# A two-layer graph kernel on one core: stores moved to the load queue, sums of B kept in memory, a third scale spread by TensorE

## The chip, the core and the metric

The kernel runs on one core of a Trainium2 chip. The metric is the device time of one execution in microseconds; the time given is the median of several runs. One execution was also taken by the hardware profiler, and the views below come from it. Engines are named as in the profile: PE is TensorE's matmul, PEld its weight load, DVE is VectorE, ACT ScalarE, POOL GpSimd and SP SyncE. The last three and the DMA engines matter here mostly through their queues[...].

## The reference, cut to what matters

```python
def _L0_gnn_ref(cur, incidence_m):
    head = (incidence_m > 0).astype(incidence_m.dtype)
    head = head / jnp.maximum(jnp.sqrt(jnp.sum(head * head, axis=-1, keepdims=True)), 1e-12)
    inc = incidence_m + head
    return (inc @ cur) / jnp.sum(inc, axis=-1, keepdims=True)

def _L1_gnn_ref(X, A, W):
    A2 = A + jnp.eye(A.shape[0], dtype=A.dtype)
    dscale = jnp.diagonal(A2) ** (-0.5)
    temp = A2 @ X @ W.T
    A_norm = dscale[:, None] * A2 * dscale[None, :]
    return jax.nn.relu(A_norm @ temp)

x = _layernorm(x + _L0_gnn_ref(x, adj))          # x: 4096 x 512, adj: 4096 x 4096, float32
x = _layernorm(x + _L1_gnn_ref(x, adj, L1_gnn_W))
```

Three large products have adj as one factor: inc @ x in layer 0, then A2 @ X and A_norm @ temp in layer 1. For layer 0 every row of adj needs the number of its positive elements before it can be used: its square root scales the 0/1 mask that is added.

## The kernel before, in words

**Stage 1, layer 0** (lines 602 to 689). The rows of adj are taken in pairs of row blocks, j and j + 16, of 128 rows each. A pair runs through four chunks (c = 0 to 3) of the other dimension. Each 2x2 arrangement of blocks is multiplied by Strassen's scheme in Winograd's form: seven products instead of eight, from sums of the four quarters. `prepare1` makes a chunk ready on VectorE one chunk ahead: raw sums for the later layers (`raw_sums`), the mask times its scale (`masks`, L449, and L456), the sums (`add_up`, L168 to L171). `multiply1` (L487) issues the 28 products of the chunk. At the end of a pair `combine` takes the seven results out of their banks, the first copies of it by ScalarE (L518, L524).

The counts are ScalarE's. `count(times)` takes that many tiles (128 x 512 elements of adj in natural order), lets `signs` (L337) add up the signs of each, for pairs from 4 on also a plain sum (L385), and asks for a further tile on SP's queue (`load_natural`, L372; five buffers). One pair has 16 tiles. How many are counted behind which chunk is written out by hand, in the tuple that `count` is given in the loop over the chunks. When a pair's 16 counts are there, `spread` makes them into a scale that lies along the free dimension: part 0 adds up and takes the root; after it there are two ways. Parts 1 and 2 multiply the identity by it on VectorE (L407) and let TensorE spread it with a matrix of ones (L422), and ScalarE copies the result out (L424). Part 3 instead stores it in DRAM and loads it back to all partitions, both on POOL's queue (L415, L417). Before the change the scales of pairs 1 and 2 go TensorE's way, pair 1's in the opening and pair 2's while pair 1 is multiplied; all later ones go by DRAM.

**Stages 2 and 3, layer 1** (from L1041). Both products, k = 2 and k = 3, are cut by Strassen's scheme twice: an outer one with seven products p, and within each an inner one of seven matmuls. So `steps` runs over k, two strips s, the seven p in the order of ORDER, and eight kk: 224 steps, each of seven matmuls (`multiply2`, L283), each matmul two instructions in the trace. Eight steps with one p are called a phase here. For each step VectorE sums the adj side (`prepare`, L168 to L171, three buffers) two steps ahead, and for every two steps (a group) it makes the inner sums of the B side (`sum_b`):

```python
t = pools["tops"].tile([P, 2, 4, P], F32, name="ts", bufs=2)
nc.vector.tensor_sub(t[:, :, 0:2, :], ...)              # L262
nc.vector.scalar_tensor_tensor(t[:, :, 2, :], ...)      # L263
nc.vector.tensor_add(t[:, :, 3, :], ...)                # L264
```

The tile of adj sums, a, is loaded by SP (`load`, L214 to L218) LA + PF steps ahead (three in k = 2, five in k = 3) into a ring of four or six buffers; the raw B, tr, is loaded by SP too (`load_b`, L255, three buffers), after every second step.

Outer sums of adj that k = 2 makes and k = 3 needs again are stored in DRAM. S1 and S3 come from layer 0. S2 and S4 are made in `prepare` of k = 2, in phases p = 6 and p = 3, from a tile r that stays in memory for the strip: `tensor_add(r, r, a)` (L237) for the last four kk, at `raises` (L249) earlier for the first four. Each is then stored by POOL's queue (L238), 1 MB, 32 times.

At the end of a phase `outer` takes the seven results out (L702 to L710). While k = 2 still runs, `project` multiplies finished row pairs by W (L784), sums the parts into rows z (L813 to L822), and `leave_operands` scales them and stores them by POOL (L837, L843) as the B side of k = 3. In k = 3 `layer1` and `layer1_first` turn finished blocks back (L858), rectify them (L862, L906), add the residual and take statistics in `rest`, one step later. `finish` then works off the last four steps by product instead of by step (L936), so that each result can be taken out while the next is multiplied.

Of the kernel before, what the change touches and what calls it, by code (L numbers as in the profile page):

```python
# [13 lines left out]
P = 128  # L14
# [12 lines left out]
def tile_adj_resnorm_d2(  # L27
# [158 lines left out]
    RAISES = {1: A11, 2: A12, 6: A11, 3: A12}  # L186
    EARLY = NQ // 2

    DONE = {(2, 7): 1, (2, 3): 0, (3, 6): 0, (3, 4): 1}
    steps = [(k, s, p, kk) for k in (2, 3) for s in range(NS) for p in ORDER[k] for kk in range(NQ)]  # L190
    groups = [st[:3] + (st[3] // 2,) for st in steps[::2]]
# [2 lines left out]
    resident, loaded, ready, raw_b, sums_b = {}, {}, {}, {}, {}  # L194
    made = {"a": 0, "s": 0, "load": 0, "load_b": 0}
    going, leaving = [], []
    queue, pairs, later, deferred, raises = [], [], [], [], []

    def fresh():

# [28 lines left out]
    def prepare(n):  # L229
        k, s, p, kk = steps[n]  # L230
        for i in range(n, len(steps) if n == len(steps) - TAIL + 1 else n + 1):
            complete(i)
        a = loaded.pop(n, None)
        r = resident[kk] if k == 2 and p != 4 and p != 7 else None
        if k == 2 and p in (3, 6):
            if a is not None:
                nc.vector.tensor_add(r, r, a)  # L237
            nc.gpsimd.dma_start(out=outer_2[s, kk, S2 if p == 6 else S4], in_=r)  # L238
            a = r
        i = made["s"]  # L240
        made["s"] += 1
        if n < len(steps) - 2:
            sm = (work, pools["work"], work)[i % 3].tile([P, 4, SW], F32, tag="s", name="s")
        else:

            sm = C_of[3][0][n - len(steps) + 2]
        add_up(sm, a)
        if k == 2 and p in (1, 2) and kk < EARLY:
            raises.append(lambda: nc.vector.tensor_add(r, r, a))  # L249
        ready[n] = a, sm  # L250
# [7 lines left out]
    def sum_b(g):  # L258

        b = raw_b[g]  # L260
        t = pools["tops"].tile([P, 2, 4, P], F32, name="ts", bufs=2)
        nc.vector.tensor_sub(t[:, :, 0:2, :], b[:, :, 0:4:3, :], b[:, :, 1:2, :].to_broadcast([P, 2, 2, P]))  # L262
        nc.vector.scalar_tensor_tensor(t[:, :, 2, :], t[:, :, 0, :], -1.0, b[:, :, 3, :], op0=ALU.mult, op1=ALU.subtract)  # L263
        nc.vector.tensor_add(t[:, :, 3, :], b[:, :, 2, :], t[:, :, 2, :])  # L264
        sums_b[g] = t

    def factors(n):

# [16 lines left out]
    def load_up_to(n):  # L285
        while made["load"] <= min(n, len(steps) - 1):
            load(made["load"])
            made["load"] += 1
# [86 lines left out]
    def count(times):  # L375
        for _ in range(times):
            if not waiting:
                return
            (j, h, t), nat = waiting.pop(0)
            if j not in counts:  # L380
                counts[j] = w1_pool.tile([P, 2, NT], F32, name="cnt")
                if j >= SUMMED:
                    totals[j] = w1_pool.tile([P, 2, NT], F32, name="tot")
            if j >= SUMMED:
                nc.scalar.activation(nat, nat, AF.Copy, accum_out=totals[j][:, h, t:t + 1])  # L385
            signs(nat, nat, counts[j][:, h, t:t + 1])
            load_natural()
# [76 lines left out]
    def prepare1(n, between=None):  # L464
        if n not in early:
            raw_sums(n, between)
        sums[n] = work.tile([P, 4, CW], F32, tag="s", name="s")
        for h in range(2):
            to_inc(n, h)
        add_up(sums[n], chunks[n])  # L470
# [177 lines left out]
    for n in range(NC, NP * NC):  # L648
        j, c = divmod(n, NC)
        if c == 0:  # L650
            if j > 1:
                C = combine(j - 1, acc)
            acc = [bank(m) for m in range(7)]
        if n + 2 >= NP * NC:
            load_up_to(n + 2 - NP * NC)
        else:
            load_chunk(n + 2)
        scales = j < NP - 1 and c == (2 if j == 1 else 1)
        if scales:
            spread(j + 1, 0)  # L660
        if n + 1 < NP * NC:
            prepare1(n + 1, between=(lambda: spread(j + 1, 1 if j == 1 else 3)) if scales else None)
        else:
            prepare(0)
        if n == NC:
            for g in range(5, NP // 2):
                build_last(g)
        multiply1(n, acc, (lambda: spread(j + 1, 2)) if scales and j == 1 else None)
        count(((6, 6, 5, 6) if j == 1 else (5, 4, 5, 2))[c])
        if j == 1 and c == 1:  # L670
            nc.vector.tensor_scalar(dscale, dscale, 1.0, None, op0=ALU.add)
            nc.scalar.activation(dscale, dscale, AF.Sqrt)
            nc.vector.reciprocal(dscale, dscale)
            nc.gpsimd.tensor_scalar(nscale, dscale, -1.0, None, op0=ALU.mult)
        if c == 1:
            layer0(j - 1, C)
        elif c == 2:
            operands(j - 1, C)
        if c == 3:
            load_rows(j)  # L680
# [367 lines left out]
    for n, (k, s, p, kk) in enumerate(steps):  # L1048
        if kk == 0:
            acc = [bank(m) for m in range(7)]  # L1050
        load_up_to(n + LA + PF)
        if n + LA < len(steps):
            prepare(n + LA)
        if n % 2 == 0 and n // 2 + 1 < len(groups):
            sum_b(n // 2 + 1)
        end = n >= len(steps) - NQ
        items = [queue.pop(0) for _ in range(min(len(queue), 2 if end else 1))] if 1 <= kk <= (6 if end else 5) else []
        held = later[:]
        later.clear()
        while deferred:  # L1060
            deferred.pop(0)()
            if not pairs:
                break
        between = {3: lambda: take_up(items.pop(0))} if len(items) > 1 else {}
        if kk in (2, 4) and pairs:
            going.append(project(*pairs.pop(0), kk == 2))
        for pair in going:
            between.update(next(pair))
        if kk == 5 and leaving:

            between[2], between[4] = leaving
            leaving.clear()
        if n < len(steps) - TAIL:
            multiply2(n, acc, between)
        if n == 0:
            layer0(NP - 1, C)
        elif n == 1:
            operands(NP - 1, C)
            parts = w_t.rearrange("(f e p) (o d) -> f o p e d", e=2, p=P, o=2)
            for op, (f, o) in {B11: (0, 0), T4: (0, 1), B21: (1, 0), B22: (1, 1)}.items():  # L1080
                nc.gpsimd.dma_start(out=wt[:, op], in_=parts[f, o])
        elif n == 4:
            outer_sums(wt[:, T1:T4 + 1], wt[:, B11], wt[:, T4], wt[:, B21], wt[:, B22])
        if n % 2 == 1 and n > 1:
            load_b_up_to(n // 2 + 3)
        for item in items:
            take_up(item)
        for rest in held:
            rest()
        for pair in going[::-1]:  # L1090
            next(pair)
        if kk in (4, 6):
            del going[:1]
        if 1 <= kk <= (6 if end else 5):
            for kind, args in queue[:2]:
                fetch(kind, *args)
        if kk == NQ - 1 and n + 1 < len(steps):
            outer(k, p, acc)
            if (k, p) in DONE:
                h = DONE[k, p]  # L1100
                if k == 2:
                    pairs.extend((h, s, i) for i in range(SB))
                else:
                    queue.extend((layer1, (h, b)) for b in blocks(h, s))
            if n == len(steps) - 1 - NQ:
                last = sorted(blocks(1, s), key=lambda b: b[1])
                queue.extend((layer1_first, (1, *last[i:i + 2])) for i in range(0, len(last), 2))
            for kind, args in queue[:2]:
                fetch(kind, *args)
        while raises:  # L1110
            raises.pop(0)()
        while kk == NQ - 1 and leaving:
            leaving.pop(0)()
        if n + 1 == len(steps) // 2:

            scope.close()
            ring3 = ctx.enter_context(tc.tile_pool(name="ring3", bufs=2))
            late["pool"] = ctx.enter_context(tc.tile_pool(name="late", bufs=1))

            root, eps_by = (late["pool"].tile([P, NB], F32, name=t) for t in ("root", "eps_by"))  # L1120
            nc.vector.reciprocal(root, dscale)
            nc.vector.scalar_tensor_tensor(eps_by, root, LN_EPS, root, op0=ALU.mult, op1=ALU.mult)
            late["root"], late["eps"] = root, eps_by
            i = made["a"] % 4
            pools["turn"] = [ring3] * 2 + pools["turn"][i:] + pools["turn"][:i]
            made["a"] = 0
            PF = 3
# [36 lines left out]
```

## Time and profile before

| | |
|---|---|
| median of 3 runs | 2284.97 us (2283.08 to 2285.19) |
| profiled execution, its own time | 2280.52 us |
| its span | 2278.7 us |
| PE busy | 2253.0 us, 99% |
| DVE busy | 1858.3 us, 82% |
| ACT busy | 536.3 us, 24% |
| POOL busy | 354.3 us, 16% |
| SP's DMA queue | 417.38 MB |
| POOL's DMA queue | 137.03 MB |

The span runs from the first to the last instruction of the core; the execution's own time has a little around it. Busy times of engines overlap, so they don't add up to the span. In the lists of waits a line reads: the engine and the tile and line that waited, the engine and line that released it, the total in us, how often, and the longest. In timelines: start, duration, engine, line, operation, what is written from what, the shapes, the count, and in brackets the idle time ahead of it with its releaser. In the tables by window each engine has its busy time and, in brackets, its number of instructions; after them come the granted clock of TensorE, the busy share of the DMA engines and the GB/s that they moved.

### The profile page before, as it was taken

The page shows a single profiled execution, that of the slowest core. Times are in us where ns is not written, and L with a number is a line of the kernel's source. Part 1 is how long each engine was busy: PE and PEld are TensorE (multiplying, and loading weights), DVE is VectorE, ACT ScalarE, POOL GpSimd, SP SyncE. Part 2 cuts the span into 40 slices and gives each one's busy share as a digit, 9 for nine tenths or more (in the row PEclk, how much of TensorE's full clock was granted, in tenths as well). Part 3 has the DMA queues.
Part 4 walks back from the last instruction along what each step waited for, and adds up shares of the span by engine and source line. Part 5 has one row for each costly group of instructions (what it writes and reads, how often), then busy time and mean ns, then how long its engine had stood idle before and what let it go on. Part 6 is the DMA issues. An engine that isn't in the chain of part 4 may idle for free.

```text
span 2278.7 us, 22117 instructions
## 1 busy us (share of the span) xinstructions
PE 2253.0 (99%) x7358; PEld 1382.7 (61%) x7359; DVE 1858.3 (82%) x2635; ACT 536.3 (24%) x1335; POOL 354.3 (16%) x500
## 2 busy tenths in 40 slices
PE   8999999999999999999999999999999999999997
PEld 6888888888888844445555444555544444444443
DVE  6988998989899787789876778887767788767787
ACT  4345545545553000000111100111110011100013
POOL 0111112211121110001333300233320000000010
PEclk9999999999999999999999999999999999999999
DMA  9787778878776576574766856577785576766572
GB/s 329 274 298 249 254 258 265 271 257 271 249 250 219 192 284 241 210 268 183 289 240 212 285 202 257 193 288 258 224 254 218 217 259 243 261 231 225 215 259 105
DMA packets 155425, 555.80 MB, mean 244 GB/s; under 512 B 17408, under 2 KB 31760, under 8 KB 116912
## 3 DMA queue, kind: packets, MB, share of 16 engines
q1 hardware_dynamic: 114624, 417.38, 51.9%
q0 software_dynamic: 40688, 137.03, 17.7%
q8 instruction: 58, 0.95, 0.2%
q14 instruction: 55, 0.45, 0.1%
HBM read 434.78 MB, written 119.55 MB: 243 GB/s over the span
## 4 chain that ended last, share of the span: by engine, by line
PE 92%; DMA 3%; DVE 3%; ACT 1%; issue 0%; SPq 0%; POOL 0%; DVEq 0%; ACTq 0%
PE q L283 56%; PE q L487 31%; PE q L784 4%; DMA nat<-adj 1%; DMA b<-x 1%; PE q L936 1%; DMA a<-adj_q 1%; DMA ob<-z 1%; ACT nat L337 0%; DVE s L168 0%; PE q L858 0%; DVE s L170 0%; DVE o L713 0%; DVE st L150 0%; DVE c L713 0%
## 5 line engine op out<-in xcount | busy, mean ns | idle before, releaser
L283 PE MATMUL q<-s,ts 128*128 128x512 f32 x1320 | 609.4, 592 | 0.0
L487 PE MATMUL q<-b,s 128*128 128x256 f32 (+1 forms) x1920 | 453.7, 379 | 0.3 <-DVE s L170 0.3
L283 PEld LDWEIGHTS q<-s,ts 128*128 128x128 f32 x1320 | 250.9, 190 | 296.8 <-issue 270.0
L168 DVE TENSOR_TENSOR s<-a 128x1024 f32<-128x1024 f32 x234 | 288.1, 1231 | 148.9 <-PE q L283 122.1
L487 PEld LDWEIGHTS q<-b,s 128*128 128x128 f32 x1920 | 363.0, 189 | 52.4 <-DVE s L170 0.7
L487 PE MATMUL q<-b,a 128*128 128x256 f32 (+1 forms) x1440 | 350.8, 379 | 1.4 <-ACT p L518 1.4
L283 PE MATMUL q<-a,tr 128*128 128x512 f32 x688 | 327.7, 593 | 2.2 <-DVE c L703 2.2
L487 PEld LDWEIGHTS q<-b,a 128*128 128x128 f32 x1440 | 272.9, 190 | 40.0 <-ACT p L518 1.9
L283 PE MATMUL q<-s,tr 128*128 128x512 f32 x440 | 224.7, 592 | 0.0
L283 PEld LDWEIGHTS q<-a,tr 128*128 128x128 f32 x688 | 129.0, 190 | 144.8 <-issue 136.6
L337 ACT ACTIVATE nat<-nat,tiny 128x512 f32<-128x512 f32 x240 | 172.9, 721 | 33.7 <-DMA nat<-adj 27.3
L283 PE MATMUL q<-a,ts 128*128 128x512 f32 x344 | 175.8, 593 | 0.0
L170 DVE TENSOR_TENSOR s<-a,s 128x512 f32<-128x512 f32 x234 | 165.6, 708 | 8.0
L171 DVE TENSOR_TENSOR s<-a,s 128x512 f32<-128x512 f32 x234 | 165.3, 706 | 8.0
L702 ACT COPY p<-q 128x512 f32<-128x512 f32 x27 | 15.7, 583 | 652.6 <-PE q L283 642.5
L449 DVE SCALAR_TENSOR_TENSOR mask<-a,sc 128x1024 f32<-128x1024 f32 (+2 forms) x129 | 154.2, 1196 | 2.1
L456 DVE TENSOR_TENSOR a<-a,mask 128x1024 f32<-128x1024 f32 x123 | 150.7, 1225 | 6.2
L283 PEld LDWEIGHTS q<-s,tr 128*128 128x128 f32 x440 | 83.7, 190 | 91.5 <-issue 82.4
L385 ACT ACTIVATE nat<-nat 128x512 f32<-128x512 f32 x192 | 118.3, 616 | 21.3 <-DMA nat<-adj 21.2
L283 PEld LDWEIGHTS q<-a,ts 128*128 128x128 f32 x344 | 65.4, 190 | 82.4 <-issue 76.9
L439 POOL DMA_DIRECT2D oa<-sr x64 | 57.7, 902 | 276.3 <-DVE sr L430 176.4
L891 POOL DMA_DIRECT2D out<-o x24 | 13.1, 545 | 532.2 <-ACT o L163 532.2
(216 smaller groups left out, 2223.9 us busy)
## 6 DMA issues: line engine op xcount, KB each, us to landing
a<-adj_r SPq DMA_DIRECT2D x112, 1024.0 KB, 6.8
a<-oa SPq DMA_DIRECT2D x80, 1024.0 KB, 5.3
nat<-adj SPq DMA_DIRECT2D x240, 256.0 KB, 6.1
a<-adj_q SPq DMA_DIRECT2D x60, 1024.0 KB, 6.1
tr<-ob SPq DMA_DIRECT2D x112, 512.0 KB, 3.9
oa<-sr POOLq DMA_DIRECT2D x64, 512.0 KB, 7.1
oa<-r POOLq DMA_DIRECT2D x32, 1024.0 KB, 9.1
y<-x POOLq DMA_DIRECT2D x64, 256.0 KB, 7.7
```

Of the source, the lines that this page charges most:

```text
L168: nc.vector.tensor_add(s[:, S3:S1 + 1, :], a[:, A11:A22 + 1, :], a[:, A21, :].unsqueeze(1).to_broadcast([P, 2, w]))
L170: nc.vector.tensor_add(s[:, S2, :], a[:, A11, :], s[:, S1, :])
L171: nc.vector.tensor_add(s[:, S4, :], a[:, A12, :], s[:, S2, :])
L283: nc.tensor.matmul(acc[m], left, right, start=(kk == 0), stop=(kk == NQ - 1))
L337: nc.scalar.activation(y, a, AF.Sign, bias=tiny, scale=2.0 ** 64, accum_out=accum)
L385: nc.scalar.activation(nat, nat, AF.Copy, accum_out=totals[j][:, h, t:t + 1])
L439: nc.gpsimd.dma_start(out=dst, in_=sr.rearrange("p m (k i) -> p (m k) i", i=P))
L449: nc.vector.scalar_tensor_tensor(m, v, 0.0, s.unsqueeze(1).to_broadcast(list(v.shape)), op0=ALU.is_gt, op1=ALU.mult)
L456: nc.vector.tensor_add(z, z, y)
L487: nc.tensor.matmul(acc[m][:, 0:w], left, b[:, right, 0:w], start=(kk == 0), stop=(kk == NP - 1))
L784: nc.tensor.matmul(ps, left[:, e, :], wt[:, right, e, :], start=(e == 0), stop=(e == 1))
L936: nc.tensor.matmul(acc[m], left, right, start=False, stop=(kk == NQ - 1))
```

## The change

It has three parts.

1. In `prepare` of k = 2 the store of S2 or S4 is no longer issued on POOL's queue at once. It is put on a list, and the next step issues it on SP's queue, after that step's load of a.
2. In `sum_b`, for the phases p = 7 and p = 4 of k = 3 (the last two in the order), the first strip stores its inner sums of B in DRAM (on POOL's queue, eight tiles of 512 KB), and the second strip loads them (on SP's queue) instead of making them on VectorE.
3. The scale of pair 3, made while pair 2 is multiplied, goes TensorE's way as that of pair 2 does, one chunk later than before (c = 2). The counts are dealt out anew: 6, 6, 5, 2 in pair 1, 5, 4, 6, 3 in pair 2, 7, 4, 5, 2 in pair 3, and 5, 4, 5, 2 from then on; before they were 6, 6, 5, 6 in pair 1 and 5, 4, 5, 2 from then on.

```diff
+    KEPT = (7, 4)
+    kept_b = {}
...
-            nc.gpsimd.dma_start(out=outer_2[s, kk, S2 if p == 6 else S4], in_=r)
+            stores.append(lambda: nc.sync.dma_start(out=outer_2[s, kk, S2 if p == 6 else S4], in_=r))
             a = r
...
         t = pools["tops"].tile([P, 2, 4, P], F32, name="ts", bufs=2)
+        k, s, p, i = groups[g]
+        sums_b[g] = t
+        if (k, s) == (3, NS - 1) and p in KEPT:
+            nc.sync.dma_start(out=t, in_=kept_b[p, i])
+            return
         nc.vector.tensor_sub(t[:, :, 0:2, :], b[:, :, 0:4:3, :], b[:, :, 1:2, :].to_broadcast([P, 2, 2, P]))
         nc.vector.scalar_tensor_tensor(t[:, :, 2, :], t[:, :, 0, :], -1.0, b[:, :, 3, :], op0=ALU.mult, op1=ALU.subtract)
         nc.vector.tensor_add(t[:, :, 3, :], b[:, :, 2, :], t[:, :, 2, :])
-        sums_b[g] = t
+        if (k, s) == (3, 0) and p in KEPT:
+            kept_b[p, i] = dram.tile([P, 2, 4, P], F32, name=f"kb{p}_{i}")
+            nc.gpsimd.dma_start(out=kept_b[p, i], in_=t)
...
-        scales = j < NP - 1 and c == (2 if j == 1 else 1)
+        scales = j < NP - 1 and c == (2 if j <= 2 else 1)
         if scales:
             spread(j + 1, 0)
         if n + 1 < NP * NC:
-            prepare1(n + 1, between=(lambda: spread(j + 1, 1 if j == 1 else 3)) if scales else None)
+            prepare1(n + 1, between=(lambda: spread(j + 1, 1 if j <= 2 else 3)) if scales else None)
...
-        multiply1(n, acc, (lambda: spread(j + 1, 2)) if scales and j == 1 else None)
-        count(((6, 6, 5, 6) if j == 1 else (5, 4, 5, 2))[c])
+        multiply1(n, acc, (lambda: spread(j + 1, 2)) if scales and j <= 2 else None)
+        count({1: (6, 6, 5, 2), 2: (5, 4, 6, 3), 3: (7, 4, 5, 2)}.get(j, (5, 4, 5, 2))[c])
...
         load_up_to(n + LA + PF)
+        while stores:
+            stores.pop(0)()
         if n + LA < len(steps):
             prepare(n + LA)
```

More of the change, by code (lines that the diff above doesn't have):

```diff
@@ L196, in tile_adj_resnorm_d2 @@
     going, leaving = [], []
-    queue, pairs, later, deferred, raises = [], [], [], [], []
+    queue, pairs, later, deferred, raises, stores = [], [], [], [], [], []
     def fresh():
```

## The prediction

> **What bounds the kernel now.** I read the page first, then TensorE's own waits, then the timelines around each of those waits. The page settles the engine:
>
> ```profile
> PE 2253.0 (99%) x7358; PEld 1382.7 (61%) x7359; DVE 1858.3 (82%) x2635; ACT 536.3 (24%) x1335; POOL 354.3 (16%) x500
> ...
> PE 92%; DMA 3%; DVE 3%; ACT 1%; issue 0%; SPq 0%; POOL 0%; DVEq 0%; ACTq 0%
> ```
>
> TensorE is busy in all but 25.7 us of the 2278.7 us span. So work taken off VectorE, GpSimd or a queue is worth nothing by itself; only a shorter stall of TensorE is. Of its idle time 6.4 us lie before the first matmul and 8.6 us after the last one; the change touches neither. What is left between, in the waits of TensorE:
>
> ```profile
> PE q L936 <- DVE c L170: 4.1, 1, 4.1
> PE q L283 <- DVE c L703: 2.2, 1, 2.2
> PE q L487 <- ACT p L518: 1.4, 1, 1.4
> PE q L858 <- ACT o L906: 0.7, 1, 0.7
> PE q L936 <- DVE ts L263: 0.6, 1, 0.6
> ```
>
> Each happens once. **Stall A** (L518) stands at 124 us, where pair 1 ends. ScalarE's timeline says why: its queue still holds the six counts of L337, which wait for their tiles, and the copy of q1 that frees a bank is queued behind them.
>
> ```profile
> 117.69 0.72 ACT L337 ACTIVATE nat<-nat,tiny 128x512 f32<-128x512 f32 x1 [1.88 <-DMA nat<-adj]
> ...
> 123.13 0.72 ACT L337 ACTIVATE nat<-nat,tiny 128x512 f32<-128x512 f32 x1 [4.63 <-DMA nat<-adj]
> ...
> 123.85 0.35 ACT L518 COPY p<-q 128x258 f32<-128x258 f32 x1
> ```
>
> From TensorE's start at 122.22 to 127.24 are 14 instructions of 0.217 us, 3.03 us; they took 5.02. A costs 1.99, not 1.45: the refill behind it is ragged too.
>
> **Stall B** (L703) stands at 1286 us: VectorE had waited 3.0 us at L818 for a z row whose store landed 12 us after its issue.
>
> **Stall C** (L170, L263) is in the last tail. First TensorE, then VectorE, then the granted clock (the column after POOL):
>
> ```profile
> 2245.78 1.12 PE L936 MATMUL q<-c,ts 128*128 128x512 f32 x2 [0.63 <-DVE ts L263]
> 2250.97 2.08 PE L936 MATMUL q<-c,ts 128*128 128x512 f32 x2 [4.07 <-DVE c L170]
> 2252.84 2.58 PE L936 MATMUL q<-s,ts 128*128 128x512 f32 x4
> 2255.25 1.88 PE L936 MATMUL q<-c,ts 128*128 128x512 f32 x4
> ```
> ```profile
> 2226.49 0.68 DVE L262 TENSOR_TENSOR ts<-tr 128x512 f32<-128x512 f32 x1
> ...
> 2244.58 0.68 DVE L262 TENSOR_TENSOR ts<-tr 128x512 f32<-128x512 f32 x1
> ...
> 2250.22 0.69 DVE L170 TENSOR_TENSOR c<-a,c 128x512 f32<-128x512 f32 x1
> ```
> ```profile
> 2250.00:2251.00 1.00, 0.03 (x1) 0.04 (x1) 0.93 (x3) 0.00 (x0) 0.00 (x0) 0.90 0.00 0
> 2251.00:2252.00 1.00, 1.00 (x2) 0.48 (x3) 1.00 (x2) 0.00 (x0) 0.00 (x0) 0.50 0.00 0
> ```
>
> VectorE is the late one here, with an inner sum of B (L262 to L264) inside its last run of work. And the wait is paid twice: the six instructions after it took 4.28 us (2250.97 to 2255.25) where six of 0.429 are 2.57, so 1.70 us more went to a clock of 0.50.
>
> [...] 4.07 us idle was followed by 0.50, the idle times of 1.45 and 2.16 us by 1.00. [...] this trace has 3.9 for tr on SP and 7.1 for the oa stores on POOL.
>
> **Part 1, counts and the third scale.** The last count of pair 1 falls from 6 tiles to 2. Two counts end at 114.4 even with their wait of 1.11, q1 is complete at about 120, so L518 finds ScalarE free: stall A goes, -1.99. Pair 3 then takes TensorE's way: two instructions of 0.217 us on TensorE (pitch at L422), **+0.43**; on VectorE two products with ident at 0.28 (L407); on ScalarE one copy of 0.37. Off POOL go two small stores of 0.55 and the 6.5 us between them. VectorE idles 2.1 us at pair 2's end (before L519), which hides its 0.6.
> What is late next: in pair 2 the copy of the scale waits for TensorE's third chunk, and behind it ScalarE now has 6+3 counts of two passes each, pitch 1.46 us: 13.1 us. The product stands a quarter of a chunk before its end, so 3.01 + 12.04 us before TensorE needs q1's bank again; the hand-over and the copy take 0.47 (from 107.48 to 107.95 in pair 1), q1's own copy 0.37, so 14.2 are there for 13.1, 1.05 spare. The sixth to ninth tile are requested only as the first to fourth leave, 5.8 us earlier, and nat lands in 6.1 (2.8 to 11.4). At the median that eats 0.3 of the spare; at 8 us about 1.1 us of stall return. I take **+0.3**, bounds 0 and +1.5. Pair 3's first chunk has 7 counts, 10.2 us, ready when VectorE reduces them (it came to L393 11 us after the pair's start). Part 1: -1.99+0.43+0.3 = **-1.26**.
>
> **Part 2, kept sums.** Eight groups lose L262, L263, L264: 8 x (0.750+0.457+0.428) = 13.1 us of VectorE, nearly all under TensorE. On the path are the three in the last phase, 1.52 us each by their pitch. The first two do not arrive: ScalarE's copy at 2228.36 (L906) waits for TensorE's transposes and stands ahead of the square root that VectorE needs, so of their 3.04 us only 0.80 pass (the root can start at 2228.87 instead of 2229.67). The third, at 2244.58, passes whole. L170 thus ends 2.3 us earlier; TensorE resumes at 2248.67. Idle is then 2.65 us (2246.0 to 2248.65)[...] and the 1.70 of half clock goes too: **-4.0**. The 0.63 at L263 vanishes into the same wait.
> Added: eight stores of 512 KB on POOL (issue near 0.9, landing near 7) whose buffer is rewritten two groups, 24 us, later, and eight loads on SP (issue 0.38). A load waits until TensorE leaves the ts buffer; so does the next 1 MB load of a, hence nothing else is held up. It has two steps, 12.0 us, and 2.1 MB ahead or with it[...]. The last one is tightest: its buffer is free at 2236.4, it is used at 2245.15; 3.9 us (12.6 at worst) for landing. Cost 0; bounds 0 and +4.0 (the tail gain lost).
>
> **Part 3, stores on SP.** 32 issues leave POOL (19.1 us), 32 come to SP (about 0.33 each, 10.6 us). Each waits on SP for VectorE's add (L237) one step back; behind it are tr and the next a, which wait for the end of the same or the next step on TensorE anyway. For tiles 0 to 3 of a phase there is no add, and no load. Stall B is not at these steps (the stores of the strip had ended 110 us before), so I leave it: 0, bounds -2.4 (B gone with its ragged refill) and +22 (the second rival).
>
> **Sum**: -1.26-4.0 = -5.3 us on the profiled execution, 2280.5 to 2275.2. That execution lies 4.5 us below the median of the runs, 2284.97; carried over, **2279.7**.
>
> **Rivals.** (1) Half a gain: pair 2's end takes over A's wait, or the last kept load lands at its worst, 12.6 us after 2236.4, that is at 2249.0, which gives C back. Then -1.3 to -4.5: 2280.5 to 2283.7. For it: both margins are about or under a typical landing's spread. Against: DMA is nearly idle in the tail (0 to 21 GB/s).
> (2) Slower: SP's queue backs up where S2 and S4 are made. In steps 4 to 7 of those four phases SP carries 1.05 MB in, 1.05 out and 0.26 of B per 6.01 us, 393 GB/s. Against 9.44 MB in 24 us, a rate R gives an excess of 9.44 MB/R - 24; VectorE's sums of the sixth step were 4.2 us ahead of TensorE (971.9, 976.1). At 280 GB/s the excess is 9.7, each phase loses 5.5, 22 in all: 2302. It outweighs the gain and 0.2% when four phases lose 9.9 us, R below about 307. Against it: those 36 us ran at 280 to 423, mean 335, already with store and load together, and on one queue the load now stands ahead of the store it competed with.
> (3) The moved stores also free the z rows: B goes, 2277.3.
>
> **How the numbers follow.** 0.2% of 2284.97 is 4.57 us, about what a measurement of this kernel can tell from no change: faster is below 2280.4, slower above 2289.5. Forecast 0.49 and rival 3 0.08, both faster: 0.57. Rival 1, with kept sums that relieve nothing in it: 0.29, same. Rival 2: 0.14. The low end takes B's removal with all of C (2275.5); the high end, 2287, takes in rival 1 and the first misses of rival 2.
>
> **What would show it.** Right: no wait at L518's line at 124 us, six instructions of q<-d,ones_f instead of four, no clock of 0.50 before the last matmul, the wait on L170 between 2 and 3 us, eight DVE triples fewer, 32 oa stores under SPq. Wrong: a new wait of TensorE on p near 171 us; on ts or on s in phases 6 and 3[...]; or a changed pitch of the matmuls.

## The result and the profile after

| | before | after |
|---|---|---|
| median of 20 runs each, same chip | 2283.45 us | 2278.78 us |
| ratio, 95% interval | | 0.9977, 0.9969 to 0.9984 |
| profiled execution, its own time | 2280.52 us | 2276.73 us |
| its span | 2278.7 us | 2275.0 us |

The kernel became faster by 4.7 us by the medians (forecast: 5.3) and by 3.8 us by the two profiled executions (forecast: 5.3). So the sign and the size were forecast well. The forecast of the median itself, 2279.7, came within 0.9 us; the kernel before had measured 1.5 us lower over 20 runs than over the three that the forecast started from. The profiled pair lacks 1.5 us, and that is what has to be explained.

In the kernel after, the code has ten lines more above the places of interest: L487 is L497 there, L283 is L293, L936 is L946, L858 is L868, L337 is L347, L518 is L528, L703 is L713, L818 is L828 and L906 is L916. The page of the kernel after, engines and chain:

```profile
PE 2252.8 (99%) x7361; PEld 1381.7 (61%) x7361; DVE 1846.3 (81%) x2613; ACT 537.0 (24%) x1336; POOL 342.0 (15%) x474
...
PE 96%; DVE 1%; DMA 1%; issue 1%; POOL 0%; ACT 0%; SPq 0%; DVEq 0%; POOLq 0%
```

VectorE lost 12.0 us and GpSimd 12.3, TensorE's busy time stayed. The waits of TensorE say what that was worth:

```profile
PE q L946 <- DVE c L170: 2.6, 1, 2.6
PE q L293 <- DVE c L713: 2.5, 2, 2.0
PE q L868 <- ACT o L916: 0.7, 1, 0.7
PE q L950 <- DVE c L1026: 0.5, 1, 0.5
```

**Stall A** is gone: no wait on p is left. ScalarE's timeline shows that it now stands idle before the copy instead of being late with it; and at the end of pair 2, where nine counts come, it arrives with no idle time, but in time:

```profile
113.06 0.72 ACT L347 ACTIVATE nat<-nat,tiny 128x512 f32<-128x512 f32 x1 [1.02 <-DMA nat<-adj]
...
119.87 0.38 ACT L528 COPY p<-q 128x258 f32<-128x258 f32 x1 [5.99 <-PE q L497]
...
169.18 0.72 ACT L347 ACTIVATE nat<-nat,tiny 128x512 f32<-128x512 f32 x1
...
169.90 0.35 ACT L528 COPY p<-q 128x258 f32<-128x258 f32 x1
```
```profile
169.05 1.89 PE L497 MATMUL q<-b,s 128*128 128x256 f32 x8
170.79 1.46 PE L497 MATMUL q<-b,a 128*128 128x256 f32 x6
172.09 1.89 PE L497 MATMUL q<-b,s 128*128 128x256 f32 x8
```

In the second fence no row of TensorE has a bracket: pair 2's end costs nothing.

**Stall C** shrank, and no half clock follows it. TensorE's timeline, and the table by window (the column with the granted clock comes after POOL):

```profile
2245.14 1.02 PE L946 MATMUL q<-c,ts 128*128 128x512 f32 x2
2248.78 1.12 PE L946 MATMUL q<-c,ts 128*128 128x512 f32 x2 [2.62 <-DVE c L170]
2249.75 1.88 PE L946 MATMUL q<-s,ts 128*128 128x512 f32 x4
```
```profile
2249.00:2250.00 1.00, 1.00 (x3) 0.46 (x3) 1.00 (x2) 0.00 (x0) 0.00 (x0) 1.00 0.00 0
2250.00:2251.00 1.00, 1.00 (x3) 0.38 (x2) 0.96 (x6) 0.00 (x0) 0.00 (x0) 1.00 0.00 0
```

**Stall B**, which no edit touches, is where the half clock stands now:

```profile
1284.67 1.50 PE L293 MATMUL q<-a,tr 128*128 128x512 f32 x2 [2.01 <-DVE c L713]
1285.97 4.10 PE L293 MATMUL q<-s,ts 128*128 128x512 f32 x6
```
```profile
1285.00:1286.00 1.00, 1.00 (x3) 0.32 (x2) 0.90 (x2) 0.00 (x0) 1.00 (x3) 0.65 0.95 295
1286.00:1287.00 1.00, 1.00 (x3) 0.48 (x2) 0.79 (x3) 0.00 (x0) 1.00 (x2) 0.50 0.95 270
1287.00:1288.00 1.00, 1.00 (x3) 0.48 (x2) 1.00 (x2) 0.00 (x0) 0.25 (x1) 0.50 0.81 265
```

Six instructions took 4.10 us there (2.74 at the full clock, as a row of B further down shows), a wait of 2.01 us ahead of them. The same stall in the kernel before had a slightly longer wait, 2.2 us, and the full clock after it (1.00 from 1286 to 1289 us).

Where TensorE didn't wait in these profiles, its instructions started at one distance (0.429 us for 128x512, about 0.217 for 128x256). What the single distances exceed that by is called the idle time by pitch here. Its sum, place by place after the first 15 us, gives the account of the two executions (us):

| place | before | after | difference | forecast |
|---|---|---|---|---|
| 74 us, opening | 0.48 | 0 | -0.48 | none |
| A, 124 us | 1.99 | 0 | -1.99 | -1.99 |
| spread's two instructions, 156 us (their own time) | 0 | 0.43 | +0.43 | +0.43 |
| pair 2's end, 171 us | 0 | 0 | 0 | +0.3 |
| L713, 1221 us | 0 | 0.70 | +0.70 | none |
| B, 1286 us | 2.4 | 4.0 | +1.6 | 0 |
| C, 2249 us | 6.73 | 2.79 | -3.94 | -4.0 |
| sum | | | -3.7 | -5.3 |

The spans differ by 3.8. The forecast's own steps held to about a tenth, but for the +0.3; what went missing lies at B and at 1221 us.

### The profile page after: what moved, and what is told of

Same layout as the page of the kernel before. It is cut to its first block, busy times and chain, and to the rows that moved or that the text cites. A ratio compares the mean times of both kernels' runs of the same rounds, so it can differ in the third digit from the quotient of the medians.

```text
span 2275.0 us, 22102 instructions
## 1 busy us (share of the span) xinstructions
PE 2252.8 (99%) x7361; PEld 1381.7 (61%) x7361; DVE 1846.3 (81%) x2613; ACT 537.0 (24%) x1336; POOL 342.0 (15%) x474
## 4 chain that ended last, share of the span: by engine, by line
PE 96%; DVE 1%; DMA 1%; issue 1%; POOL 0%; ACT 0%; SPq 0%; DVEq 0%; POOLq 0%
PE q L293 56%; PE q L497 32%; PE q L794 4%; PE q L510 2%; DMA ob<-z 1%; PE q L946 1%; PE q L868 0%; POOL ob L847 0%; DMA a<-adj_q 0%; PE q L363 0%; PE q L358 0%; DVE s L168 0%; DVE o L723 0%; DVE st L927 0%; DVE c L168 0%
## 5 line engine op out<-in xcount | busy, mean ns | idle before, releaser
L293 PE MATMUL q<-s,ts 128*128 128x512 f32 x1320 | 610.7, 593 | 0.0
L497 PE MATMUL q<-b,s 128*128 128x256 f32 (+1 forms) x1920 | 453.4, 378 | 0.0
L293 PEld LDWEIGHTS q<-s,ts 128*128 128x128 f32 x1320 | 251.2, 190 | 298.3 <-issue 271.6
L497 PEld LDWEIGHTS q<-b,s 128*128 128x128 f32 x1920 | 362.7, 189 | 52.0
L497 PE MATMUL q<-b,a 128*128 128x256 f32 (+1 forms) x1440 | 350.5, 379 | 0.0
L293 PE MATMUL q<-a,tr 128*128 128x512 f32 x688 | 328.1, 593 | 2.0 <-DVE c L713 2.0
L497 PEld LDWEIGHTS q<-b,a 128*128 128x128 f32 x1440 | 272.7, 189 | 38.3
L293 PE MATMUL q<-s,tr 128*128 128x512 f32 x440 | 224.7, 592 | 0.0
L293 PEld LDWEIGHTS q<-a,tr 128*128 128x128 f32 x688 | 128.8, 190 | 144.8 <-issue 137.3
L347 ACT ACTIVATE nat<-nat,tiny 128x512 f32<-128x512 f32 x240 | 172.9, 721 | 31.7 <-DMA nat<-adj 25.4
L293 PE MATMUL q<-a,ts 128*128 128x512 f32 x344 | 175.8, 592 | 0.0
L293 PEld LDWEIGHTS q<-s,tr 128*128 128x128 f32 x440 | 83.6, 190 | 91.6 <-issue 83.0
L293 PEld LDWEIGHTS q<-a,ts 128*128 128x128 f32 x344 | 65.3, 190 | 82.5 <-issue 76.8
L801 POOL TENSOR_TENSOR y<-c,c 128x256 f32<-128x256 f32 x16 | 21.5, 1347 | 518.1 <-DVE c L727 387.4
## 6 DMA issues: line engine op xcount, KB each, us to landing
oa<-r SPq DMA_DIRECT2D x32, 1024.0 KB, 10.1
```

The lines of the kernel that those rows point to most:

```text
L293: nc.tensor.matmul(acc[m], left, right, start=(kk == 0), stop=(kk == NQ - 1))
L347: nc.scalar.activation(y, a, AF.Sign, bias=tiny, scale=2.0 ** 64, accum_out=accum)
L497: nc.tensor.matmul(acc[m][:, 0:w], left, b[:, right, 0:w], start=(kk == 0), stop=(kk == NP - 1))
```

## The experiments

Two questions. First: is each part worth what it was put at, by itself? Second: what decides that a half clock follows a stall? The theory at first was the prediction's (the length of the idle time decides); the rival, which the profile above suggests, is that something else does. All ratios are to the kernel before on the same chip, whose median was 2283.13 to 2283.99 us in the comparisons. Not all comparisons ran on one chip, so kernels from different ones are set against each other by these ratios.

**Part 1 alone.** The kernel before with the counts and the third scale of the change:

```diff
-        scales = j < NP - 1 and c == (2 if j == 1 else 1)
+        scales = j < NP - 1 and c == (2 if j <= 2 else 1)
...
-        count(((6, 6, 5, 6) if j == 1 else (5, 4, 5, 2))[c])
+        count({1: (6, 6, 5, 2), 2: (5, 4, 6, 3), 3: (7, 4, 5, 2)}.get(j, (5, 4, 5, 2))[c])
```

> The kernel before with the counts and the third scale of the change alone (part 1). My theory: the idle time at pair 1's end (1.45 us in the waits, 1.99 by the pitch) is gone, two more instructions of TensorE cost 0.43, pair 2's end shows no wait; TensorE's idle in the tail stays near 4.1 us at the first matmul that reads c. So 1.1 to 1.6 us faster than before. Rival, that stall A's removal is given back at pair 2's end: a wait of TensorE on p near 170 us, and 0 to 0.5 us faster.

Measured: 2282.53 us (13 runs) against 2283.99, ratio 0.9994 (0.9986 to 1.0002). Stall A is gone, pair 2's end has no wait, and C with its half clock stays at 4.1. All of TensorE's waits above 0.7 us after the first 15 us:

```profile
PE q L936 <- DVE c L170: 4.1, 1, 4.1
PE q L283 <- DVE c L703: 2.8, 2, 2.5
PE q L487 <- DVE s L170: 1.3, 1, 1.3
```

In the profiled execution the gain is hidden by longer stalls elsewhere: by pitch 0.9 us more than before in the opening, at 74 us, 0.4 more at 1222 us and 0.3 more at B. The opening's place shows 0 to 1.8 in the twelve profiles, with no edit there. The size of -1.3 us fits; the interval reaches from -3.2 to +0.5, so it is the trace that shows part 1's worth, not the time.

**Part 2 alone.** The kernel before with the sums of B kept for p = 7 and p = 4:

```diff
+        if (k, s) == (3, NS - 1) and p in KEPT:
+            nc.sync.dma_start(out=t, in_=kept_b[p, i])
+            return
...
+        if (k, s) == (3, 0) and p in KEPT:
+            kept_b[p, i] = dram.tile([P, 2, 4, P], F32, name=f"kb{p}_{i}")
+            nc.gpsimd.dma_start(out=kept_b[p, i], in_=t)
```

> The kernel before with the kept sums alone (part 2). My theory: this is most of the gain, 3.5 to 4.2 us: the wait on c in the tail falls from 4.1 to about 2.6 us and no half clock follows it; stall A stays at 1.4. Rival, that the gain in the tail came from the loads being off GpSimd's queue or from the run's luck with the clock: [...] gain under 2 us.

Measured: 2280.56 us (21 runs), ratio 0.9986 (0.9978 to 0.9993): 3.4 us by the medians, where 3.5 to 4.2 had been expected, with an interval from 1.6 to 5.0. The wait at C is 2.6 us with the full clock after it, as in the kernel after. But B's wait of 2.0 us drew a half clock in this execution too, without part 1 and part 3.

**Part 3 alone.** The kernel before with the stores of S2 and S4 on SP's queue, one step later:

```diff
-            nc.gpsimd.dma_start(out=outer_2[s, kk, S2 if p == 6 else S4], in_=r)
+            stores.append(lambda: nc.sync.dma_start(out=outer_2[s, kk, S2 if p == 6 else S4], in_=r))
...
+        while stores:
+            stores.pop(0)()
```

> The kernel before with S2 and S4 stored on SP a step later, alone (part 3). My theory: 0, within 1 us; stalls A, B and C as before, the loads of a in phases 6 and 3 no later for TensorE. Rival 1: SP's queue backs up, TensorE waits on s or r in phases 6 and 3, slower by 3 us or more. Rival 2: less work on GpSimd's queue lets the z rows leave sooner, the wait for them at the row sums (9.8 us in all before) falls, B goes, 2 us faster.

Measured: 2283.49 us (14 runs), ratio 1.0002 (0.9994 to 1.0011): no difference. A, B and C stand where they stood, and no wait on s or r was added. A was 2.7 us long here and was followed by a half clock, as the rows by window show. So a stall of 2.7 us can draw it at A, and one of 2.6 at C did not.

```profile
123.00:124.00 1.00, 0.00 (x0) 0.00 (x0) 0.00 (x0) 0.08 (x1) 0.00 (x0) 1.00 1.03 379
124.00:125.00 1.00, 0.00 (x0) 0.00 (x0) 0.00 (x0) 1.00 (x4) 0.00 (x0) 0.78 0.82 305
125.00:126.00 1.00, 0.96 (x2) 0.83 (x3) 0.88 (x4) 1.00 (x4) 0.00 (x0) 0.50 0.40 137
```

**Only the last sum of B kept.** The prediction held that of the three triples in the last phase the first two stop at ScalarE's copy, and only the third passes whole. Here the kernel before keeps only that one:

```diff
+        if (k, s) == (3, NS - 1) and (p, i) == (4, 3):
...
+        if (k, s) == (3, 0) and (p, i) == (4, 3):
```

> The kernel before with one kept sum alone, that of the last group; all others are made on VectorE. My theory says that of the sums before it only 0.8 us reach TensorE because ScalarE's copy stands in the way: the wait on c falls by 1.5 (last triple), to about 3.3 to 3.4 us counted from the end of the matmul before, with the 0.6 at the sums of B gone; whether the half clock follows is open[...]. So 1.5 us faster if it does and 3.2 if it does not. Rival, that all the triples of the last phases count alike: the wait falls by little, 0.5 us faster.

Measured: 2282.56 us (14 runs), ratio 0.9991 (0.9983 to 1.0). TensorE's wait at C and the clock after it:

```profile
2249.70 1.13 PE L946 MATMUL q<-c,ts 128*128 128x512 f32 x2 [3.44 <-DVE c L170]
```
```profile
2250.00:2251.00 1.00, 1.00 (x3) 0.38 (x2) 0.97 (x2) 0.00 (x0) 0.00 (x0) 1.00 0.00 0
```

3.44 against 2.62 with all kept: the first two triples together, 3.04 us of VectorE, are worth 0.82 us, and the prediction had put them at 0.80. And a wait of 3.44 us was followed by the full clock. That is one execution, the fastest of the 14; the medians differ by 1.4 us.

**C's wait filled.** To measure the half clock by itself, the kernel before keeps its sums and gives TensorE 14 more products with the identity, whose result nobody reads, inside C's wait:

```diff
-        multiply(q6)
+        multiply(q6, slice(0, TAIL - 1))
+        fill = spare()
+        for _ in range(14):
+            nc.tensor.matmul(fill[:, 0:P], ident, ident, start=True, stop=True)
+        multiply(q6, slice(TAIL - 1, TAIL))
```

> The kernel before with 14 spare products of the identity put into TensorE's wait in the tail, ahead of the last kk of q6; their result is not used, nothing else changes. They take 28 x 0.109 = 3.1 us of a wait of 4.1. My theory: the wait on c ends where it did, the half clock of 3.4 us behind it does not come, 1.7 us are won at that place. Rival, that the slow instructions behind the wait are a refill and not the clock: nothing is won, they stay at 0.85 us apart.

Measured: 2281.69 us (14 runs) against 2283.13, ratio 0.9995 (0.9987 to 1.0003). After the filled wait the matmuls start 0.429 us apart at once, so the half clock's 1.70 us are gone from that place, with VectorE as late as ever; the time agrees (-1.4) but its interval reaches +0.7:

```profile
2250.76 3.29 PE L982 MATMUL q<-ident 128*128 128x128 f32 x28
2254.99 1.13 PE L936 MATMUL q<-c,ts 128*128 128x512 f32 x2 [0.95 <-DVE c L170]
2255.96 1.88 PE L936 MATMUL q<-s,ts 128*128 128x512 f32 x4
```

In the same execution B waited 3.8 us and kept its full clock:

```profile
1290.22 1.12 PE L283 MATMUL q<-a,tr 128*128 128x512 f32 x2 [3.82 <-DVE c L703]
1291.18 2.74 PE L283 MATMUL q<-s,ts 128*128 128x512 f32 x6
```

**What is behind the wait that was left.** In the kernel after VectorE idles 4.10 us at 2229 us, for a square root of ScalarE that stands behind the copy L916. In the kernel before the wait for the same root was 0.36 us, so most of what the first two kept triples freed turned into waiting there:

```profile
2228.52 0.60 ACT L916 ACTIVATE o<-q 128x512 f32<-128x512 f32 x1 [3.14 <-PE q L868]
2229.02 0.28 ACT L154 ACTIVATE sd<-mv,eps_t 128x1 f32<-128x1 f32 x1
2229.34 0.16 DVE L160 RECIPROCAL rs<-sd 128x1 f32<-128x1 f32 x1 [4.10 <-ACT sd L154]
```

Here the kernel after lets the held sums of the step before (`rest`) go ahead of the step's own blocks in the last phase:

```diff
-        for item in items:
-            take_up(item)
-        for rest in held:
-            rest()
+        if end:
+            for rest in held:
+                rest()
+            for item in items:
+                take_up(item)
+        else:
...
```

> The changed kernel, with the rests of the step before (statistics and normalising) issued ahead of the copies of the new blocks in the last phase. My theory says that the first two kept sums of the last phase did not reach TensorE because ScalarE's copy, which waits for TensorE, stands ahead of the square root: VectorE's wait of 4.1 us for that root goes, TensorE's wait on c in the tail falls from 2.6 to under 1 us, 1.8 to 2.5 us faster than the changed kernel. Rival, that VectorE's own work is what is left: the wait on c falls by less than 0.5.

Measured: 2276.42 us (9 runs), ratio 0.9971 (0.9962 to 0.9981). VectorE's wait fell to the root's own time, C's wait of TensorE is gone, and the wait at L868 grew from 0.7 to 1.3:

```profile
2226.95 0.17 DVE L160 RECIPROCAL rs<-sd 128x1 f32<-128x1 f32 x1 [0.36 <-ACT sd L154]
```
```profile
PE q L293 <- DVE c L713: 3.9, 1, 3.9
PE q L868 <- ACT o L916: 1.3, 1, 1.3
```

So the order of issue was behind C's wait, as the prediction had read it: with the root ahead of the copy VectorE comes in time. The edit reorders the work of both engines; that it is ScalarE's copy that held the root is what the rows above show. Against the kernel after the medians differ by 2.4 us (1.8 to 2.5 expected), but the ratios' intervals overlap, so it is the trace that shows the gain, not the time. B's wait in this execution was 3.9 us, and a half clock followed.

**The third scale by DRAM again,** with the new counts; this takes TensorE's two instructions away and keeps pair 1's short last count:

```diff
-        scales = j < NP - 1 and c == (2 if j <= 2 else 1)
+        scales = j < NP - 1 and c == (2 if j == 1 else 1)
...
-        count({1: (6, 6, 5, 2), 2: (5, 4, 6, 3), 3: (7, 4, 5, 2)}.get(j, (5, 4, 5, 2))[c])
+        count({1: (6, 6, 5, 2), 2: (9, 4, 5, 2)}.get(j, (5, 4, 5, 2))[c])
```

> The changed kernel, but the third scale goes by DRAM as before: pair 1 counts 6, 6, 5, 2 and pair 2 counts 9, 4, 5, 2. My theory: stall A stays gone, since it was the four counts at pair 1's end that made it; the two instructions of 0.217 us go, 0.4 us faster than the changed kernel, which only the records of TensorE can tell. Rival, that TensorE's way was needed: the 9 counts come late, VectorE waits at the reduce and TensorE for s in pair 2, 1 us or more slower.

Measured: 2276.92 us (10 runs), ratio 0.9971 (0.9962 to 0.998), which can't be told from the kernel after. A stays gone and pair 2 has no wait. So what removed A was the last count of pair 1; the way of the third scale added 0.43 us and bought nothing that the trace shows. C's wait was again 2.62 us, and here the half clock came:

```profile
2247.58 2.07 PE L946 MATMUL q<-c,ts 128*128 128x512 f32 x2 [2.62 <-DVE c L170]
2249.45 2.37 PE L946 MATMUL q<-s,ts 128*128 128x512 f32 x4
```

The same wait, for the same tile, at 0.429 us a matmul in one execution and 0.86 in the other.

**B itself.** VectorE waits at L828 for the buffer of a z row whose store is late. In the kernel after it reads:

```profile
1277.80 0.42 DVE L828 TENSOR_TENSOR z<-p,p 128x256 f32<-128x256 f32 x1 [2.85 <-DMA ob<-z]
```

Here the kernel after has the two stores issued earlier in their step, at its matmuls 0 and 2 instead of 2 and 4:

```diff
-            between[2], between[4] = leaving
+            between[0], between[2] = leaving
```

> The changed kernel, with the first row pair's scaling and stores of a step issued at its matmuls 0 and 2 instead of 2 and 4. My theory: stall B comes from the z row, which the second row pair can only write when those stores have landed; they leave 1.3 to 2.2 us sooner, VectorE's wait for the z row falls from 2.9 to about 1 us, TensorE's loss there (2.2 to 2.5 us, with a half clock 1.6 more) falls below 0.8: 1.5 to 3 us faster. Rival, that the stores are slow because the loads of a run beside them: they land when they did, nothing is won.

Measured: 2272.82 us (6 runs), ratio 0.9956 (0.9943 to 0.9969). VectorE no longer waits for the z row:

```profile
1274.91 0.42 DVE L828 TENSOR_TENSOR z<-p,p 128x256 f32<-128x256 f32 x1
```

TensorE's wait at B is gone, and that at 1221 us with it. By the ratios it is 4.8 us faster than the kernel after, by the medians, which come from two comparisons, 6.0; 1.5 to 3 had been expected. The same edit in the kernel before, without anything of the change:

> The kernel before with one edit: the two stores of the z rows offered at hooks 0 and 2 of step 5 in place of 2 and 4; nothing of the change. Theory (the stall at 1286 us is independent of the change, and the change left it as it was): the wait of TensorE on L703's tile at 1286 us goes, -2.3 us, and with it the half clock that can follow it; the stalls at 122 us (1.6) and at 2249 us (4.2 and the half clock) stay as in before. Median 2280.3 (from 2283.3), ratio 0.9987, range 0.998 to 0.999. Rival (the change's moved stores of S2 and S4, which left POOL's queue, are what let the early z rows pay): the z store waits on POOL's queue behind the other stores, the wait at 1286 us stays over 1 us, and the ratio is within 0.9995 to 1.0005.

Measured: 2278.39 us (13 runs) against 2283.54, ratio 0.998 (0.9971 to 0.9988). B's wait is gone here too, while A and C (with a half clock) stay:

```profile
PE q L936 <- DVE c L170: 4.1, 1, 4.1
PE q L487 <- ACT p L518: 1.8, 1, 1.8
```

So B does not depend on S2's and S4's stores. Its gain of 5.1 us by the medians, 2.7 to 6.6 by the interval, is again more than the 2.4 us that the profile of before shows at B.

**All together.** The kernel after with the early z rows, the held sums first, and the third scale by DRAM:

> The kernel after with three more edits together: the two stores of the z rows offered at hooks 0 and 2 of step 5 in place of 2 and 4; in the last phase the held sums (the rests) ahead of the last triple's own; and the third pair's scale again spread through DRAM, with counts (6, 6, 5, 2) and (9, 4, 5, 2). Theory (the three act on different stalls, so their gains add): from the profile of the kernel with the early z rows, whose excess pitch was 6.46 us, the wait of 2.79 us at the last phase's start goes and the root wait at L868 grows by 0.65: 4.3 us left, profiled 2270.6, median 2270.5, ratio 0.9945, with no wait of TensorE over 1.5 us after the first 15 us. Rival 1 (no cover left at the end: with the rests first, the last root of VectorE is late and the end waits): the wait at the last identity product grows from 0.68 to 2 us or more, median 2272.5. Rival 2 (DRAM's scale comes late in pair 2 again, as in the kernel before): a wait of 1.6 to 2 us with L487's successor at about 122 us or 170 us, median 2272.5 too, but told apart by its place.

Measured: 2269.63 us (5 runs) against 2283.54, ratio 0.9939 (0.9926 to 0.9953). The waits of TensorE that are left after the first 15 us, all of them:

```profile
PE q L497 <- DVE s L170: 1.6, 1, 1.6
PE q L868 <- ACT o L916: 1.3, 1, 1.3
PE q L950 <- DVE c L1026: 0.5, 1, 0.5
```

The first is the opening's, 1.6 where 0.5 had been counted on; neither rival shows (L950 at 0.5, no wait at 122 or 170 us).

## Why the prediction was right or wrong

**The counts (-1.99) and the two instructions (+0.43)** came out to the hundredth in the profiled pair. For A that says only that nothing of it remained, since its size was read from the same profile. **The re-stall at pair 2's end (+0.3)** measured 0: the tiles came in time, with 0.3 us of waiting among nine counts. The term was too careful, as was its bound of 1.5.

**The kept sums (-4.0)** measured -3.94: the wait of 2.62 (forecast 2.65), the 0.63 at L263 gone, the half clock gone. The split of the three triples is shown by two experiments. The margin of the last kept load held: no wait on ts is left. The eight loads landed in 7.7 us at the median (5.2 to 9.2). But the step from 2.65 us of idle time to "the 1.70 of half clock goes too" **reached the right number for this execution by a wrong rule, and so by luck**. The length of the idle time alone doesn't decide: 3.44 us at C and 3.8 us at B left the full clock; 2.01 us at B and 2.74 us at A took it away; and the same 2.62 us at C was followed by the full clock in the kernel after and by the half clock with the third scale by DRAM.

**Stall B (0)** is the failed term: +1.6. It was right that none of the parts touches B. It was wrong that an untouched stall costs the same each time: its wait was 2.0 to 3.9 us in the nine profiles that have it, of kernels that issue the same work there but for S2's and S4's stores, and a half clock followed in three of them. The wait at 1221 us (0 to 1.7 us) is of the same kind; it went with B's. Of the prediction's six signs of being right this one failed: "no clock of 0.50 before the last matmul". The other five came.

**The moved stores (0)** measured 0. The second rival, SP's queue backing up, was to outweigh the gain below 307 GB/s. In the stretch that the prediction had looked at, the sixth step of such a phase and around it, the kernel after moved more than that (last column), with TensorE busy throughout (first):

```profile
960.00:966.00 6.00, 6.00 (x16) 2.65 (x15) 3.12 (x4) 0.00 (x0) 0.00 (x0) 1.00 0.98 356
966.00:972.00 6.00, 6.00 (x16) 2.65 (x15) 5.79 (x6) 0.00 (x0) 0.00 (x0) 1.00 1.03 397
972.00:978.00 6.00, 6.00 (x15) 2.65 (x14) 4.61 (x6) 0.00 (x0) 0.00 (x0) 1.00 0.98 380
978.00:984.00 6.00, 6.00 (x15) 2.66 (x14) 5.76 (x8) 0.00 (x0) 0.00 (x0) 1.00 1.03 410
```

The first rival (a stall taken over at pair 2's end or by a late load) didn't occur; the third (B goes with the moved stores) is refuted by part 3 alone.

**Why the medians still fell by 4.7.** An estimate from two figures measured in the last section: if 2.2 us of idle time in one window of 3.41 always draw a half clock in the next, as in the cases of its table, and if the place of a stall in the windows is random, a stall of length g draws one with a chance of (g + 3.41 - 2 x 2.2)/3.41. That is 0.95 for C before (4.23 us by pitch) and 0.53 after (2.79); the first switch of the clock, at 9.7 to 12.7 us in the twelve profiles (11.7 before, 12.1 after), does differ by most of a window. On average part 2 is then worth 2.24 + 0.42 x 1.70 = 3.0 us, not 3.9. With -1.99 and +0.43 the estimate is 4.5 us, where 4.7 was measured. A scatters too: by pitch 1.7 to 2.4 us in five of the six profiles that have it, and 4.4 in the one with a half clock; with their mean, 2.5, the estimate is 5.0. The forecast's 5.3 counted the whole 1.70 as saved, and the profiled pair lost 1.6 more at B. The two gains of the early z rows (4.8 and 4.6 us by the ratios, more by the medians) are larger than this estimate gives for B and 1221 us (3 to 4 us): some 1 to 2 us there, within the intervals, stay unexplained.

## What to carry to other kernels

Cost a short stall of TensorE in two terms: its length, and the half clock after it, here 1.7 us times a chance that by the estimate above grows with the length. Both scatter (at B the wait was 2.0 to 3.9 us), and one profiled execution shows one draw of them, so compare several before a microsecond is put down to an edit. When VectorE is late at a place, look back along its waits for the queue that holds it: here work taken off it paid only behind its last wait for ScalarE (0.8 us of 3.0), and a changed order of issue removed the wait altogether. And when a bounding engine is busy for 99%, list every stall and price the ones that a change does not touch as well: the largest gain here was in one of those, for one line.

## What the runs showed of the hardware

**The clock switched on a fixed grid.** In the profile of the kernel before the granted clock switched at 11.67, 2250.81, 2254.22 and 2271.29 us, in that of the kernel after at 12.12, 1285.29, 1288.71 and 2268.33, the last time after the final matmul. The distances are 656, 1 and 5 times 3.4133 us, and 373, 1 and 287 times. In the other ten profiles too all switches lay whole multiples of it apart (to about 0.001 of a multiple). A stretch of 3.4133 us between two borders of this grid is called a window here; a half clock lasted one window, once two. The idle time of TensorE by pitch, cut at the borders and added up in each window after the first 20 us, parted the cases of these profiles so:

```
idle us in one window       half clock in the next window
2.05  2.09  2.15  2.15      no   (nor in more than 30 windows with 0.9 to 2.0)
2.22  2.28  2.30  2.41      yes
2.96  2.99  3.08  3.10 3.41 yes
```

The 3.41 is C in the kernel before, the 2.28 B in the kernel after. The switches at 2271.29 and 2268.33, behind the last matmul, followed windows with 2.24 and 2.98 us idle. The most without a half clock was 1.61 in the kernel before (at A) and 1.86 in the kernel after (at C).

The 3.44 us of the kernel that keeps one sum fell 1.84 and 1.87 into two windows by pitch, the 3.8 us at B 2.15 and 1.94: no half clock. The 2.01 us at B in the kernel after lay whole in one window, which ended at 1285.29: half clock. One window that was itself at half clock, with 1.5 us idle, was followed by another. The border in these cases lies between 2.15 and 2.22 us, about two thirds of a window; it rests on these few.

**A stall's cost scattered without any edit,** and the profiles show it at B (2.4 us by pitch before, 4.0 after). The times only fit it: 20 runs of the kernel before reach from 2280.1 to 2292.7 us, five runs of the last kernel, which has no wait over 1.6 us, from 2269.1 to 2271.4; but the ten runs with the third scale by DRAM, which has both B and C, lie as close, from 2275.0 to 2277.7.

**A store of 1 MB landed no sooner from SP's queue:** 10.1 us at the median after, 9.1 before from POOL's; in the kernel after it is also issued a step later, behind a load. What moved was 32 issues of GpSimd's time, which bounded nothing.
